# A two-layer Fourier-operator attention kernel: from woven stages to 1748 recorded units issued in one planned order

## The chip, the cores and the metric

The kernel runs on one core of one Trainium2 chip, as a single launch, with all data in float32. The metric is device microseconds of one execution; three executions of the kernel before took 553.83, 553.83 and 556.35 us, median 553.83. The profiled execution is a further one, recorded with the hardware profiler.

## The reference

The input x is 2 images x 56 rows x 128 x 128. Two layers of the same form follow each other, with weights of their own. Each adds to x an attention block on spectral convolutions, applied to a group-normalised x:

```python
def _gn(v, G=32, eps=1e-5):        # mean and variance over 56, 128 and groups of 4 of the last axis
    ...
def spectral_conv(x, w, b):        # keeps 32 x 16 Fourier modes
    xf = jnp.fft.rfft2(x, norm='forward')
    top = jnp.einsum('bihw,iohw->bohw', xf[:, :, :M1, :M2], _c(w[0]))
    bot = jnp.einsum('bihw,iohw->bohw', xf[:, :, -M1:, :M2], _c(w[1]))
    ...
    y = jnp.fft.irfft2(of, s=(H, W), norm='forward')
def fno_layer(x, w, b, sw, sb, norm=False, act=False):
    y = spectral_conv(x, w, b)     # inorm: over an image's 128 x 128 plane, norm only for M0, M1
    if norm: y = inorm(y)
    y = y + skip1x1(x, sw, sb)
    if act: y = jax.nn.gelu(y, approximate=False)
    return y
# the block, on xa = x.reshape(B * K, 1, H, W), K = 56 tokens an image, 8 heads
xn = inorm(xa, g1, b1)
k, q, v = (fno_layer(xn, ...) for K, Q, V)
scores = jnp.einsum('baks,bals->bakl', qh, kh) * scale   # s runs over the 128 x 128 plane
attn = jax.nn.softmax(scores, axis=-1)
out = fno_layer(einsum('bakl,bals->baks', attn, vh) ..., Pw, Pb, Psw, Psb)
att = inorm(out + xa, gan, ban)
an = inorm(att, g2, b2)
h = fno_layer(an, M0w, M0b, M0sw, M0sb, norm=True, act=True)
h = fno_layer(h, M1w, M1b, M1sw, M1sb, norm=True, act=False)
y = inorm(h, gmo, bmo) + att
# the program
x = x + _L0_conv_ref(_gn(x), ...)
x = x + _L1_conv_ref(_gn(x), ...)
```

## The kernel before

**What it computes instead.** K, Q and V are never formed in space. Scores, values and norms are worked out from the 32 x 16 modes of each token and from one 56 x 56 matrix per image, the Gram matrix of the normalised tokens (the sum over the whole plane of products of two tokens). Only the gelu and the result are full planes.

**Tiles.** `X2` [128, 2 images, 64, 128] holds x: two halves of the image rows on partitions 0 to 55 and 64 to 119, and each half has eight spare partitions behind it, which are filled at the start from x; the first of them (56 and 120) later holds a row that carries the bias, written at L564. `P0` and `P1` [128, 8192] are a plane of each image with the last axis on the partitions; P is used again as a room for the attention's parts, and then for h. `WU`, `WT` and `WM` hold the mode matrices of the weights, `tc` their factors, `C` the constants (transform matrices, identity, masks), `xr` three rooms of 1024 columns for x read back from DRAM, `store` a DRAM tensor for x between the layers. PSUM is two pools that rotate: `bank` (2 buffers of 512 columns) and `pair` (3 buffers of 1024).

**The steps**, one function each, for layer L and image b:

- `turned` (L363 and L365 transposes on TensorE, L368 and L371 copies on ScalarE, L373 VectorE's statistics): turns x from X2 into P, eight turnings an image.
- `prepare` (L270 to L302, VectorE and GpSimd): the weights become spectral factors. `relay` (L320 to L335): TensorE transposes, VectorE spreads (L324) and TensorE matmuls move the factors to the partitions of their modes, ScalarE copies them out (L335). `build` (L341, GpSimd, 1024 columns an instruction) and `build_m` (L348) widen them into WU, WT and WM.
- `modes_chain` (L460 to L513): mean and variance, the root on ScalarE (L468, Sqrt) and VectorE's reciprocal, scaling of P in four parts (L479 ScalarE, L481 VectorE), the row transform L485, VectorE's 32x32 transposes L490, the column transform L386, the modes `xf`; L495 writes a 128x1 column for the scale; L505 are two DMAs of `xs`, a copy of the modes on other partitions.
- `gram` (L521): 128 steps an image, each a matmul of 64 weight columns by 56 columns, on two column groups in turn, all into one bank. `gram_chain` (L531 to L554): folding, diagonal, root.
- `scale_x` (L560): VectorE scales X2 in eight pieces of 1024 columns an image, on 120 partitions; L564 are two DMAs that write that extra row.
- `scores` (L588, L607), `values` (L630), `softmax_chain` (L647 to L665), `mix_chain` (L673 to L690), `heads` (L700), `norms_chain` (L712 to L753; ScalarE Square L715, Sqrt L731): the attention on modes; `multiply` (L419), `spread`, `sums` (L441, L443) and `inverse` (L401, L406) are its helpers.
- `gelu`: `synthesis` (L761, inverse transform into two pairs) and `mixed` (L776, the skip from X2); Gelu on ScalarE (L829, 1024 columns), the statistics of h on VectorE (L831, two of 512 columns), transposes L811 (`turn_back`), ScalarE's copy L812, row transform L799 (`forward`), copy L804. Eight such pieces an image.
- `h_chain` (L845 to L890; Sqrt L869, L876): the norms of M1 from modes and from the statistics of h.
- `end`: `synthesis` and `mixed` again, VectorE's `scalar_tensor_tensor` (L926), the residual on GpSimd (L928), stores and loads of x through SyncE's queue (`moved`, L906). In layer 0 `turned` follows piece by piece, for layer 1. In the last image of layer 1 the eight pieces of x are loaded ahead into X2's room of image 0.

**Order.** Each step is a generator that yields a cost in microseconds; `_woven(lead, *bulks)` issues from the bulk until the cost that the lead gave is used up. Engines and buffers are fixed in the code. The main sequence is a fixed list of such pairs, for example, in each layer:

```python
_run(_woven(chain(modes_chain(L, 1, stats[1], s1), more), gram(0, s0)))
build(WTv, tcs, 16, range(0, 8, 2))
build_m(tcs)
_run(_woven(gram_chain(L, 0, s0), _with(gram(1, s1), scale_x(0, s0))))
...
_run(_woven(norms_chain(L, 1, s1), gelu(L, 0, s0)))
_run(_woven(h_chain(L, 0, s0), gelu(L, 1, s1)))
```

Each engine works through its own queue in the order of issue, so this order also fixes each engine's.

Of the kernel before, what the change touches and what calls it, by code (L numbers as in the profile page):

```python
# [22 lines left out]
for _name, _n in (  # L50
    ("ident", N), ("fw", 32), ("fh", N), ("gw", N), ("group", N), ("dup", N), ("ext", N), ("fold", 64),
    ("raw", 56), ("count", 2), ("syn", 1), ("same", 32), ("m8", 8), ("m16", 16), ("n2", 1), ("fx", N), ("gh", 2 * N),
):
    _PARTS[_name] = (sum(n for _, n in _PARTS.values()), _n)
# [3 lines left out]
def _constants():  # L58
# [25 lines left out]
    dup, ext, fold = np.zeros((N, N)), np.zeros((N, N)), np.zeros((N, 64))  # L84
    for r in range(2):
        dup[k, 64 * r + k] = 1
        ext[k, 64 * r + k] = 1
        ext[k, 64 * r + K] = -1
        fold[64 * r + k, k] = 1
# [16 lines left out]
        "ident": np.eye(N), "fw": fw, "fh": fh, "gw": gw, "group": group, "dup": dup, "ext": ext,  # L106
# [4 lines left out]
        "m8": (p[:, None] % 8 == np.arange(8)) * 1.0,  # L111
        "m16": (p[:, None] // 8 == np.arange(16)) * 1.0,
# [3 lines left out]
    return {"all": np.ascontiguousarray(whole, np.float32)}  # L116
# [24 lines left out]
def _woven(lead, *bulks):  # L141

    rest = chain(*bulks)
    for want in lead:
        while want > 0:
            cost = next(rest, None)
            if cost is None:
                break
            yield cost
            want -= cost  # L150
    yield from rest


def _with(bulk, extra):

    for cost in bulk:
        next(extra, None)
        yield cost


def _run(units):
    for _ in units:
        pass
# [3 lines left out]
def fno_layers(ctx: ExitStack, tc: tile.TileContext, x, out, weights, small, const):  # L167
    nc = tc.nc
    V, S, G, T = nc.vector, nc.scalar, nc.gpsimd, nc.tensor
    pool = lambda name, bufs, **kw: ctx.enter_context(tc.tile_pool(name=name, bufs=bufs, **kw))  # L170
    cp = pool("const", 1)
    xp = pool("x", 1)
    pp = pool("plane", 1)
    wp = pool("mats", 1)
    sp = pool("modes", 1)
    sm = pool("small", 1)
    dp = pool("dram", 1, space=bass.MemoryType.DRAM)
    ps = pool("psum", 2, space=bass.MemoryType.PSUM)
    pq = pool("pair", 3, space=bass.MemoryType.PSUM)

    def bank():
        return ps.tile([N, 512], F32, name="bank")

    def pair():
        return pq.tile([N, 2, 512], F32, name="pair")

    def little(name, shape):
        return sm.tile(shape, F32, name=name)
# [3 lines left out]


    Ct = cp.tile([N, N_CONST], F32, name="C")
    C = {k: Ct[:, o : o + n] for k, (o, n) in _PARTS.items()}
    ident = C["ident"]
    nc.scalar.dma_start(out=ident, in_=const["all"][:, :N])
    stage = cp.tile([N, 1632], F32, name="stage")
    nc.scalar.dma_start(out=stage[:, :1088], in_=weights[0].rearrange("p m r n t -> p (m r n t)"))
    smt = [cp.tile([N, N_SMALL], F32, name=f"sm{n}") for n in range(2)]  # L200
    for n in range(2):
        nc.scalar.dma_start(out=smt[n], in_=small[n : n + 1, :].to_broadcast([N, N_SMALL]))
    nc.scalar.dma_start(out=Ct[:, N:], in_=const["all"][:, N:N_CONST])
    X2 = xp.tile([N, B, 64, N], F32, name="X2")
    xin = x.rearrange("b k (g c r) w -> c b k g (r w)", c=2, r=8)
    for b in range(B):
        for g in range(0, 8, 2):
            for c in range(2):
                nc.sync.dma_start(
                    out=X2[64 * c : 64 * c + K, b, 8 * g : 8 * g + 16, :].rearrange("p (g r) w -> p g (r w)", r=8),  # L210
                    in_=xin[c, b, :, g : g + 2, :],
                )
    for b in range(B):
        nc.sync.dma_start(out=X2[K:64, b], in_=x[b, :8, :64, :])
    eps = cp.tile([N, 1], F32, name="eps")
    V.memset(eps, EPS)
    ones = cp.tile([N, N], F32, name="ones")
    V.memset(ones, 1.0)
    P = [pp.tile([N, 8192], F32, name=f"P{b}") for b in range(B)]
    plane = [t[:, : N * K].rearrange("p (i k) -> p i k", i=N) for t in P]  # L220
    WU = wp.tile([N, 4096], F32, name="WU")
    WT = wp.tile([N, 4096], F32, name="WT")
    WM = wp.tile([N, 1024], F32, name="WM")
    WUv, WTv = (t.rearrange("p (t a m) -> p t a m", t=8, a=HEADS) for t in (WU, WT))
    WMv = WM.rearrange("p (n t m) -> p n t m", n=2, t=8)

    FB = [WU[:, 1792 * b : 1792 * b + 1792] for b in range(B)]
    half = [WT[:, 2048 * b : 2048 * b + 2048] for b in range(B)]
    hT = [WT[:, 2048 + 896 * j : 2944 + 896 * j].rearrange("p (r e c k) -> p r e c k", r=2, e=4, c=2) for j in range(2)]
    xr = cp.tile([N, 3, 1024], F32, name="xr")  # L230
    G.memset(xr.rearrange("p a b -> p (a b)"), 0.0)
    store = dp.tile([B, K, N, N], F32, name="store")


    def prepare(layer, first, second):

        sml = smt[layer]
        par = {n: sml[:, o : o + k] for n, (o, k) in _COLS.items()}
        raw = stage[:, :1088].rearrange("p (m r n t) -> p m r n t", m=2, r=2, n=N_W)
        cpt = stage[:, 1088:1376].rearrange("p (n t) -> p n t", t=8)  # L240
        rawc = C["raw"].rearrange("p (k t) -> p k t", k=7)
        W, M = raw[:, 0], raw[:, 1]
        Wf = W.rearrange("p r n t -> p (r n) t")
        der = little(f"der{layer}", [N, 48])
# [8 lines left out]
        tt, ts = second.tensor_tensor, second.tensor_scalar  # L253
        ss, vp = col("ss", 8), col("vp", 8)
        tt(ss, par["s_q"], par["s_k"], ALU.mult)
        tt(vp, par["s_p"], par["s_v"], ALU.mult)
        g2 = col("g2")
        tt(g2, par["g1"], par["g1"], ALU.mult)
        ts(col("score_g", 8), ss, g2, 1.0 / N, ALU.mult, ALU.mult)
        ts(col("mix", 8), vp, par["g1"], None, ALU.mult)  # L260
        tt(col("A0"), par["g2"], par["gan"], ALU.mult)
        tt(col("A02"), d["A0"], d["A0"], ALU.mult)
        tt(col("A0m0"), d["A0"], par["m0sw"], ALU.mult)
        ts(col("gan2"), par["gan"], par["gan"], EPS, ALU.mult, ALU.add)
        ts(col("dc0"), par["m0sw"], par["b2"], par["m0sb"], ALU.mult, ALU.add)
        tt(col("bb"), par["ban"], par["bmo"], ALU.add)
        tt(col("gm1"), par["gmo"], par["m1sw"], ALU.mult)
        tt(col("m12"), par["m1sw"], par["m1sw"], ALU.mult)
        tt(col("m2"), par["m1sw"], par["m1sw"], ALU.add)
        first.tensor_tensor(Wf, Wf, _bc(rawc[:, 0], 1, 2 * N_W), ALU.mult)  # L270
        first.tensor_tensor(M, M, _bc(rawc[:, 1:3], 2, N_W), ALU.mult)
        first.tensor_tensor(W, W, M, ALU.add)
        first.tensor_tensor(W[:, 0, 0:32, :], W[:, 0, 0:32, :], _bc(sml[:, 0:32], 2, 8), ALU.add)
        rooms = (stage[:, 1376:1632], stage[:, 544:800])

        def part(r, n):
            return W[:, r, 8 * n : 8 * n + 8, :]

        def place(e, t64, to, re, im, k):

            n = re.shape[1]
            m0, m1 = _bc(rawc[:, k], 1, n), _bc(rawc[:, k + 1], 1, n)
            u, v = (t[:, :n] for t in t64[2:])
            e.tensor_tensor(u, re, m0, ALU.mult)
            e.tensor_tensor(v, im, m1, ALU.mult)
            e.tensor_tensor(to[:, :, 0], u, v, ALU.subtract)
            e.tensor_tensor(u, im, m0, ALU.mult)
            e.tensor_tensor(v, re, m1, ALU.mult)
            e.tensor_tensor(to[:, :, 1], u, v, ALU.add)

        def product(e, room, o, a, b, conj, minus, scale, k):
            t64 = [room[:, 64 * n : 64 * n + 64].rearrange("p (a t) -> p a t", a=8) for n in range(4)]
            re, im, u = t64[:3]
            e.tensor_tensor(re, part(0, a), part(0, b), ALU.mult)
            e.tensor_tensor(u, part(1, a), part(1, b), ALU.mult)
            e.tensor_tensor(re, re, u, ALU.add if conj else ALU.subtract)
            e.tensor_tensor(re, re, _bc(minus, 2, 8), ALU.subtract)
            e.tensor_tensor(im, part(0, a), part(1, b), ALU.mult)
            e.tensor_tensor(u, part(1, a), part(0, b), ALU.mult)
            e.tensor_tensor(im, im, u, ALU.subtract if conj else ALU.add)  # L300
            for t in (re, im):
                e.tensor_scalar(t, t, scale, None, ALU.mult)  # L302
            place(e, t64, cpt[:, o : o + 16].rearrange("p (a c) t -> p a c t", c=2), re, im, k)
            return t64

        product(first, rooms[0], 0, 1, 0, True, ss, g2, 3)
# [148 lines left out]
    def new_stats(b):  # L455
        return little(f"stats{b}", [N, 16, 6])
# [578 lines left out]
```

## Time and profile before

| | |
|---|---|
| median of three executions | 553.83 us |
| span of the profiled execution | 548.9 us; 4.9 us of the median lie outside a span of this length |
| TensorE (PE) busy | 440.6 us, 80%, 6438 records |
| weight loads (PEld) | 296.4 us, 54% |
| VectorE (DVE) | 350.6 us, 64%, 593 instructions |
| ScalarE (ACT) | 189.6 us, 35%, 238 instructions |
| GpSimd (POOL) | 180.4 us, 33%, 198 instructions |
| DMA | 41.00 MB in 18477 packets; read 24.68 MB, written 14.68 MB |

The span runs from the first instruction to the last. Busy time counts no register, semaphore or DMA-issuing instruction, and the ends of matmuls are modelled, so a busy TensorE is not TensorE at its peak. A float32 matmul shows as two records of TensorE. L926 is line 926 of the kernel before. The page's slices are 40 equal parts of the span with the busy share in tenths; `PEclk` is the granted TensorE clock in the same way. The chain that ended last is followed back from the last instruction, at each step to what released it.

### The profile page before, as it was taken

What the parts mean: (1) busy time and instruction counts of PE and PEld (TensorE: products, weight loads), DVE (VectorE), ACT (ScalarE), POOL (GpSimd) and SP (SyncE); (2) the same over time, 40 slices, a digit from 0 to 9 for tenths busy, and PEclk for the clock granted to TensorE, in tenths of its full rate; (3) what the DMA queues carried; (4) which work ended last, traced back from release to release, by engine and by line L of the source; (5) the groups of instructions that cost most, each with busy time, mean ns of one, the idle gap of its engine ahead of it and who ended that gap; (6) DMA issues with size and microseconds to landing.
All of it is one profiled execution on the core that took longest, in us unless ns stands there. A gap on an engine that the chain in (4) does not pass through costs nothing.

```text
span 548.9 us, 14430 instructions
## 1 busy us (share of the span) xinstructions
PE 440.6 (80%) x6438; PEld 296.4 (54%) x6438; DVE 350.6 (64%) x593; ACT 189.6 (35%) x238; POOL 180.4 (33%) x198
## 2 busy tenths in 40 slices
PE   2548879899989999789688948899998999977480
PEld 1423748768675555445563447577775555534340
DVE  0575579934547676869459994761636867767670
ACT  2333232064545557142102313224546457502000
POOL 2460325900082000155366771440000000044484
PEclk9998797999998999996667958989998999979696
DMA  8992000050000000065144641121000000027597
GB/s 209 220 221 28 10 2 11 7 148 3 2 3 1 1 2 1 1 198 172 51 132 117 187 116 32 13 69 41 4 1 2 1 1 3 1 60 225 181 219 289
DMA packets 18477, 41.00 MB, mean 75 GB/s; under 512 B 4704, under 2 KB 5472, under 8 KB 18400
## 3 DMA queue, kind: packets, MB, share of 16 engines
q1 hardware_dynamic: 17696, 38.71, 26.0%
q10 hardware_dynamic: 720, 1.38, 1.0%
q8 instruction: 50, 0.82, 0.6%
q14 instruction: 11, 0.09, 0.1%
HBM read 24.68 MB, written 14.68 MB: 72 GB/s over the span
## 4 chain that ended last, share of the span: by engine, by line
PE 46%; DVE 30%; ACT 8%; issue 7%; POOL 4%; DMA 3%; POOLq 1%; ACTq 0%; DVEq 0%
PE pair L776 8%; PE pair L761 5%; PE pair L811 5%; DVE X L560 4%; DVE stats L373 4%; PE bank L521 4%; PE bank L700 3%; DMA C<-const_all 3%; DVE P L926 3%; PE bank L485 3%; PE bank L588 3%; PE bank L799 2%; DVE WT L406 2%; PE bank L386 2%; POOL P L928 2%
## 5 line engine op out<-in xcount | busy, mean ns | idle before, releaser
L926 DVE SCALAR_TENSOR_TENSOR P<-P,hs,pair 128x1024 f32<-128x1024 f32 x32 | 40.0, 1268 | 18.8 <-PE pair L776 18.8
L831 DVE BATCH_NORM_STATS2 stats<-P 128x6 f32<-128x512 f32 x64 | 40.5, 680 | 17.3 <-ACT P L829 17.1
L928 POOL TENSOR_TENSOR X<-P,xr 128x1024 f32<-128x1024 f32 x16 | 39.3, 2462 | 32.1 <-DVE P L926 20.2
L373 DVE BATCH_NORM_STATS2 stats<-P 128x6 f32<-128x448 f32 x64 | 35.7, 612 | 20.9 <-ACT P L371 10.6
L560 DVE TENSOR_TENSOR X<-X,gvr 120x1024 f32<-120x1024 f32 x32 | 49.0, 1560 | 0.0
L829 ACT ACTIVATE P<-pair 128x1024 f32<-128x1024 f32 x32 | 32.6, 1026 | 33.0 <-PE pair L776 32.4
L521 PE MATMUL bank<-P 128*64 128x56 f32 (+1 forms) x1024 | 40.5, 250 | 0.0
L776 PE MATMUL pair<-X,Be 57*64 57x512 f32 x256 | 40.1, 726 | 0.0
L521 PEld LDWEIGHTS bank<-P 128*64 128x64 f32 (+1 forms) x1024 | 38.9, 164 | 2.2 <-issue 1.9
L395 POOL MEMSET WT<- 128x256 f32 x4 | 1.3, 314 | 114.5 <-PE bank L799 88.8
L811 PEld LDWEIGHTS pair<-C,P 120*128 120x128 f32 x256 | 27.3, 145 | 21.3 <-issue 11.5
L776 PE MATMUL pair<-X,Bs 57*64 57x512 f32 x256 | 38.4, 641 | 0.0
L761 PE MATMUL pair<-C,WT 32*128 32x128 f32 x512 | 29.3, 336 | 11.1 <-DVE P L926 5.3
L761 PEld LDWEIGHTS pair<-C,WT 32*128 32x128 f32 x512 | 24.0, 229 | 23.4 <-issue 9.3
L811 PE MATMUL pair<-C,P 120*128 120x120 f32 x256 | 35.2, 281 | 0.1
L341 POOL TENSOR_TENSOR WT<-tc,C 128x1024 f32<-128x1024 f32 x8 | 26.5, 3343 | 20.1 <-ACT tc L335 11.0
L812 ACT COPY WT<-pair 128x896 f32<-128x896 f32 x32 | 28.8, 905 | 11.8 <-PE pair L811 11.5
L363 PE MATMUL pair<-C,X 56*128 56x56 f32 x256 | 17.4, 291 | 17.5 <-DMA X<-x 11.9
L371 ACT COPY P<-pair 128x896 f32<-128x896 f32 x16 | 14.4, 901 | 45.7 <-PE pair L365 45.7
L363 PEld LDWEIGHTS pair<-C,X 56*128 56x128 f32 x256 | 14.9, 197 | 24.0 <-DMA X<-x 10.0
L365 PE MATMUL pair<-C,X 120*128 120x120 f32 x128 | 20.3, 312 | 9.2 <-POOL X L928 9.2
L365 PEld LDWEIGHTS pair<-C,X 120*128 120x128 f32 x128 | 16.1, 163 | 21.2 <-POOL X L928 11.6
(260 smaller groups left out, 880.2 us busy)
## 6 DMA issues: line engine op xcount, KB each, us to landing
X<-x SPq DMA_DIRECT2D x16, 448.0 KB
xr<-x SPq DMA_DIRECT2D x32, 224.0 KB
store<-X SPq DMA_DIRECT2D x32, 224.0 KB
out<-P SPq DMA_DIRECT2D x32, 224.0 KB
xr<-store SPq DMA_DIRECT2D x16, 224.0 KB
X<-store SPq DMA_DIRECT2D x16, 224.0 KB
C<-const_all ACTq DMA_DIRECT2D x1, 618.0 KB
stage<-weights ACTq DMA_DIRECT2D x1, 544.0 KB
```

What stands on the lines that cost most here:

```text
L363: T.transpose(p[:, c, o : o + K], X2[q, b, i, :], ident[q, q], tile_position=(64 * c, 0))
L365: T.transpose(p[:, s, N * e : N * e + 120], X2[:120, b, i, :], ident[:120, :120])
L373: V.bn_stats(stats[:, 2 * g + s, :], dst[:, 448 * s : 448 * s + 448])
L521: T.matmul(p[u : u + m, :K], lhsT=P[b][:, K * i : K * i + m], rhs=plane[b][:, i, :], start=(i < 2), stop=(i == N - 1), tile_position=(0, u ...
L560: V.tensor_tensor(v, v, _bc(st["gvr"][:120], 1, 8), ALU.mult)
L761: T.matmul(both[j // 2][:, j % 2, N * e : N * e + N], lhsT=Z[32 * j : 32 * j + 32, o : o + N], rhs=C["gw"][32 * j : 32 * j + 32, :], start ...
L776: T.matmul(p[64 * c : 64 * c + 64, r, :], lhsT=Bs[q, :], rhs=X2[q, b, s : s + 4, :].rearrange("p e w -> p (e w)"), start=False, stop=True, ...
L811: T.transpose(p[:, r, N * e : N * e + 120], h3[:120, o : o + N], ident[:120, :120])
L829: S.activation(h3, both[v].rearrange("p r m -> p (r m)"), AF.Gelu)
L831: V.bn_stats(stats[:, 4 * A + 2 * v + r, :], h3[:, 512 * r : 512 * r + 512])
L926: V.scalar_tensor_tensor(h3, h3, st["hs"], both[v].rearrange("p r m -> p (r m)"), ALU.mult, ALU.add)
L928: G.tensor_tensor(dst, h3, back(n), ALU.add)
```

## The change

The whole scheduling is replaced. The steps no longer issue instructions but write units into a book: each unit is one instruction, or a run of matmuls into one PSUM place, with the engines on which it could run. Lists in the file then give the order of all 1748 units, an engine for each, and a PSUM bank for each place; the units are played in that order under a manual schedule. PSUM is one tile of eight banks.

```diff
+class _Book:
+    ...
+    def play(self, order, chosen, at):
+        for n in order:
+            u = self.units[n]
+            e = chosen.get(n, u.kind[0])
+            for ways in u.calls:
+                op, args, kw = ways[e]
+                args = [self.to_ap(v, at) for v in args]
+                kw = {k: self.to_ap(v, at) for k, v in kw.items()}
+                getattr(self.engines[e], op)(*args, **kw)
+    ...
+_ORDER = (
+    "734F05000s4s8q4p4K5m3X6l063U7I5h07080a090c0b0e0d0Z020V011011120W170f0X0Y1318031a19141b150p161f1c0l1d1e1g1j0h1h"
+    ...
+_ENGINES = (
+    "ADDDDDDDDDDDDDDDDDDDDDDDDDDDVGGGVGGVVGGGVGGVGVVVGVVGVGGVGPVVVPSVVPSVVPSVVPSVVPSVVPSVVPSVVPSVVPSVVPSVVPSVVPSVVP"
+    ...
+_BANKS = (
+    ...
+    with tc.manual_schedule():
+        book.play(*_planned(book))
```

The engine letters are V VectorE, G GpSimd, S ScalarE, P TensorE, and D and A for DMAs issued by SyncE and by ScalarE. Since every instruction is issued from `play`, they all have one line in the profile after (the `getattr` line), and are told apart there by engine, operation and tile.

The steps themselves change in these places. Roots go to GpSimd as a power of -0.5, in place of ScalarE's Sqrt and VectorE's reciprocal:

```diff
-        S.activation(gv, gv, AF.Sqrt, bias=eps)
-        V.reciprocal(gv, gv)
+    def over_root(to, of):
+        G.tensor_tensor(to, of, C["power"][: of.shape[0]].to_broadcast(list(of.shape)), ALU.pow)
+        ...
+        over_root(gv, gv)
```

There are 20 of them. The factors no longer pass through TensorE; they are written to a DRAM tile and read back on other partitions, in four writes and 64 small reads over both layers, on SyncE or ScalarE:

```diff
-            pa = bank()
-            T.transpose(pa[:rows, :N], cpt[:, o : o + n, :].rearrange("p n t -> p (n t)"), ident)
-            ...
+        to = relay[layer][part]
+        dma("DA", to, cpt)
+        ...
+                    dma("DA", tcs[part][q : q + 8], far[c, e_, j])
```

The Gram step becomes two matmuls of 32 weight columns, by 56 and by 28 columns, on four column groups in turn; the part that is left out is the mirror of one that is there, and five small matmuls with the constants "low" and "high" put it together:

```diff
-            T.matmul(
-                p[u : u + m, :K], lhsT=P[b][:, K * i : K * i + m], rhs=plane[b][:, i, :], start=(i < 2),
-                ...
+            u, v = 32 * (i % 4), 32 * ((i + 2) % 4)
+            mm(p[u : u + 32, :K], P[b][:, o : o + 32], P[b][:, o : o + K], i < 2, i >= N - 4, tile_position=(0, u))
+            ...
+            mm(
+                p[v : v + m, K : K + 28], P[b][:, o + 28 : o + 28 + m], P[b][:, o + 28 : o + K], i < 2, i >= N - 4,
+                tile_position=(0, v),
+            )
```

The second moment of h comes from a Square on ScalarE with a running sum, which writes its squares over the PSUM pair that the Gelu read; its mean comes from the modes:

```diff
+                S.activation(h3, flat, AF.Gelu)
+                S.activation(flat, h3, AF.Square, accum_out=sq[:, n : n + 1])
```

Wide elementwise steps are cut into halves of 512 columns that may run on GpSimd or VectorE, and the scaling of X2 now covers the extra rows, since the spare partitions are filled with ones from a constant (four DMAs of together 1 MB):

```diff
-        for s in range(0, 64, 8):
-            v = X2[:120, b, s : s + 8, :]
-            V.tensor_tensor(v, v, _bc(st["gvr"][:120], 1, 8), ALU.mult)
-            ...
+        for s in range(0, 64, 4):
+            v = X2[: 64 + K + 1, b, s : s + 4, :]
+            tt("GV", v, v, _bc(st["gvr"][: 64 + K + 1], 1, 4), ALU.mult)
...
-                G.tensor_tensor(dst, h3, back(n), ALU.add)
+                for r in range(2):
+                    o = slice(512 * r, 512 * r + 512)
+                    tt("GV", dst[:, o], h3[:, o], back(2 * n + r), ALU.add)
+                    if not ahead:
+                        load(2 * n + r + 3)
```

`build` is one instruction for each of the eight parts, on either engine, and WM half as large, built once for each use; `xr` is three rooms of 512 columns that share their space with the weights' stage; the copies out of PSUM may be ScalarE's or VectorE's; the small duplicating matmuls use the identity instead of a constant `dup`. At the start x of image 0 is loaded ahead of the other constants, image 1 behind them. In all, the kernel's counts go from 3558 to 4040 matmuls, from 164 to 273 DMAs issued by SyncE and from 5 to 31 by ScalarE, and from 20 to 4 loads of an activation table.

## The prediction

> **What bounds the kernel now.** I read first the page's engine shares, its slices and its shares of the chain that ended last.
>
> ```profile
> PE 440.6 (80%) x6438; PEld 296.4 (54%) x6438; DVE 350.6 (64%) x593; ACT 189.6 (35%) x238; POOL 180.4 (33%) x198
> ...
> PE   2548879899989999789688948899998999977480
> ...
> PEclk9998797999998999996667958989998999979696
> ...
> PE 46%; DVE 30%; ACT 8%; issue 7%; POOL 4%; DMA 3%; POOLq 1%; ACTq 0%; DVEq 0%
> ```
>
> TensorE is busy 80% of the span, yet it carries less than half of the chain; VectorE carries 30%. The PE digits sag in slices 1 to 4, 17 to 24 and 36 to 40, and the granted clock falls to 0.5 in the second of these. So it is not one engine that is full: there are dense stages and thin ones. The busy times by stage say which:
>
> ```profile
> 105.00:226.00 121.00, 110.76 (x1702) 73.84 (x1697) 74.84 (x153) 63.07 (x78) 21.92 (x53) 0.99 0.07 18
> 226.00:327.00 101.00, 77.78 (x668) 47.93 (x665) 78.80 (x105) 21.48 (x29) 56.92 (x32) 0.75 0.45 129
> 482.00:549.00 67.00, 37.72 (x456) 20.69 (x448) 37.39 (x44) 3.58 (x7) 37.60 (x17) 0.80 0.65 199
> 0.00:42.00 42.00, 16.30 (x177) 11.87 (x180) 19.41 (x56) 13.46 (x14) 18.18 (x67) 1.00 0.91 215
> ```
>
> (window, its length, then busy PE, PEld, DVE, ACT, POOL; clock; DMA share; GB/s.) Attention and gelu of layer 0 (105 to 226) are a PE stage; the end of layer 0 with the modes of layer 1 (226 to 327) has PE and DVE both at 78 of 101 us, taking turns; the first 42 us wait for DMA, and the last 67 for DMA, DVE and POOL.
>
> Busy PE counts latency, so for a floor I take the pace of records back to back, from the chain in order of time (start, us, what):
>
> ```profile
> 97.57 2.87 PE bank L521 x81
> ...
> 171.67 1.10 PE pair L761 x32
> ...
> 257.59 2.35 POOL X L928
> 259.94 9.56 issue
> 269.54 3.85 POOL WU L341 x2
> ...
> 438.88 1.02 PE pair L776 x8
> 439.90 0.97 PE pair L811 x8
> ...
> 442.86 0.52 PE bank L799 x8
> ```
>
> One matmul is two records. Records by pace: L776 512 x 1.02/8 = 65.3; L761 1024 at 1.10 for 32 = 35.2; L811 256 x 0.97/8 = 31.0; the Gram sum L521 1024 x 2.87/81 = 36.3; L607 1024 at 1.08 for 64 = 17.3; L630 18.2, L588 16.0, L700 16.2, L401 16.6, L799 16.6, L365 15.5, L485 13.8, L386 13.2, L363 11.3, L419 8.8, L690 7.7, by the same view; small ones about 20. That is 359, and 13 for the relay matmuls (L320, L331): 372 us, 68% of the span. In 105 to 226 the same sum is 102.5 of 121 us, a fill of 0.85. So 177 us of the span are holes, and most lie outside that stage.
>
> **The change, part by part.**
>
> *PE work.* All but two kinds stay, record for record. The relay goes (13 us, and with it the hole at 260 to 273 where PE waits for POOL's sum and then the build). The Gram sum becomes 1024 matmuls of 32 weight columns by 56 or 28, on four column groups, for 512 of 64 by 56 on two. Lower bound: four lanes for two and 84 columns for 56 per step, 36.3 x 84/56 x 2/4 = 27.2 us. Upper: every record keeps its 35 ns, 72.6. The weight columns per step stay 64, so I take 36.3, no gain. A rule speaks for the upper end: the Trainium skill, TensorEngine Tiling (Array Packing), Instruction Overhead, gives each matmul an overhead of some 60 cycles and says not to tile a dimension that is small already. No run here shows 28 columns; by that rule the sum is that of the rival "split Gram" below. So the floor after is 359.
>
> *ACT.* 20 table loads become 4: 16 x 1.283 = 20.5 us less. Square on ScalarE is new: nearest rows L829 (1.026 for 1024 columns) and L715 (0.58 for 448), so 1.05 each, 32 x 1.05 = 33.6. Of the copies 13 of 32 at L812 (0.905) go to DVE, and 28 DMA issues come at 0.49 (L202's): 13.7. ACT stays near 195. In the gelu stage ACT has 1.03 + 1.05 + 0.54 = 2.6 us for each eighth of a plane, PE 0.55 + 1.02 + 0.97 + 0.52 = 3.06. PE hides it, by 0.4 us only; the PSUM pair is held one Square longer.
>
> *DVE.* Gone: BN statistics of h 40.5, relay spreads L324 8.7, 30.7 of the row scaling (32 at 1.56 become 29 halves at 0.63), half of L804 4.9, small ones 2. New: 20 builds x 0.63 = 12.6, 27 residual halves x 0.63 = 17, 23 evictions of 896 columns at about 1.2 (twice L804's 0.61 for 448) = 27, others 9. 350.6 becomes about 329.
>
> *POOL.* Residual 37 x 1.18 = 44 (it was 76.6), scaling 35 x 1.18 = 41 (new), builds 16 x 1.07 = 17; near 155. The 20 roots are POW on one to three columns. The trace shows no POW: bounds 0.1 us (the smallest POOL row) and 7.9 (its largest, L341); nearest is L495, a 128x1 operation at 0.65, against 0.30 + 0.16 for Sqrt and reciprocal and 1.28 where a table was loaded. I count them at nothing. What they add is a place in POOL's queue, behind TENSOR_TENSORs of 1.07 to 1.18 us.
>
> *SP.* 273 issues for 164. In the end of layer 0: 64 x 0.70 + 32 x 0.355 = 56 us of issuing for 34 before; PE's own 41 us there no longer stand alone, since the turnings of X2 are spread into layer 1's attention in the order. The relay's 68 small DMAs (28 of them ACT's) lie beside PE work. Weights, constants and the rows of ones (1 MB) now lie between the two images, so image 1 lands some 10 us later; image 0's Gram sum covers that, and without that cover it is 10 us. The eight row DMAs at L564 go, as scaling takes the row of ones along.
>
> *The sum.* Head: x of image 0 comes first, 3.67 MB at 215 GB/s = 17 us behind a small constant, and DVE no longer stands behind `prepare` (its statistics ended at 34.0). Last turning and statistics at 22; mean to shift 2.8 as now (34.0 to 36.8); scaling on three engines and four L485 groups 7; Gram sum, cold at first, 9: done at 42, where before it ended at 77. PE work done by then: L363 11.3, L485 3.5, Gram 9, L386 1.7 = 25. Tail: from the first L926 of layer 1 to the end it was 486.8 to 548.9, 62 us. Image 0's pass takes 12, spectrum 20 (23 now, roots without tables), image 1's 15 (POOL 8 x 2.35 = 18.9 now), last DMA and end 7: 54. The bytes alone, 14.7 MB at some 300 GB/s (199 at a share of 0.65), need 49. PE work in it: 37. Between lie 359 - 25 - 37 = 297 us of PE work. One order over all engines means, if it holds, that every stage is filled like the best one: 297/0.85 = 349. Sum 42 + 349 + 54 = 445 of span. The profiled execution is 548.9 of span against a median of 553.83, so 4.9 lie around it: **about 450 us**. Ends: fill 0.95, head 39, tail 48: 405; fill 0.78 with head 42 and tail 55: 483.
>
> **The rivals.**
>
> *The shared port.* Scaling and builds ran beside each other at 88 to 98:
>
> ```profile
> 88.32 10.60 POOL L341 TENSOR_TENSOR WT<-tc,C 128x1024 f32<-128x1024 f32 x4 [11.02 <-ACT tc L335]
> 89.43 7.68 DVE L560 TENSOR_TENSOR X<-X,gvr 120x1024 f32<-120x1024 f32 x3
> ...
> L560 DVE TENSOR_TENSOR X<-X,gvr x32: 1196/1211/3355, 79.1 to 362.8; 120x1024 f32<-120x1024 f32 x32
> ...
> L341 POOL TENSOR_TENSOR WT<-tc,C x8: 1942/2922/7930, 88.3 to 352.0; 128x1024 f32<-128x1024 f32 x8
> ```
>
> Alone they take 1.21 and 1.94 us, together 2.9 each: the sum, not the longer. The change puts 88 such POOL operations beside 76 such DVE ones. If each DVE one waits for a POOL one of 1.1 us, DVE carries 329 + 84 = 413; at a fill of 0.85 that is 486 + 5 = **491**. For it: these rows. Against: the total on both engines, 150 us, is that of before, and the order can keep them apart. The Trainium skill, SBUF — State Buffer, Who interferes with whom, says that this port pair is locked for a whole instruction and the loser blocks; the trace agrees (2.92 for 1.94).
>
> *Split Gram.* Upper bound above: 36.3/0.85 = 43 more, **493**. For it: L443's one-column matmul lasts 0.20 us against L521's 0.25. Against: matmuls on other column groups overlap (eight L799 records of 224 columns in 0.52).
>
> *The plan slips.* Durations differ from those the order was made for, and the fill stays at 0.68: 297/0.68 = 437, + 42 + 62 + 5 = **546**, little gained.
>
> *Slower: roots behind the lock.* A root waits in POOL's queue behind a TENSOR_TENSOR that the port holds up (7.93 at worst), DVE waits for the root, and PE for DVE, with no other PE work ordered in front. 20 x 7.9 = 158: 450 + 158 = **608**. It passes the time of before from 5.2 us a root. For it: L341's maximum and in-order queues. Against: only a few of these rows are over 3 us, and two images give PE other work.
>
> **How the numbers follow.** Forecast 0.60, port 0.13, split Gram 0.07, slip 0.10, slower 0.10. Forecast, port and split Gram hold 0.80: range 405 to 510, the upper end being 493 and half of the step from a fill of 0.85 to 0.78 (32 us), some 510. Runs of this kernel differ by 0.5% (553.83 to 556.35), which is what a measurement can tell. Faster by more: 0.88 (0.02 of the slip lands at no change), same 0.02, slower 0.10.
>
> **What would show it.** In the profile after: statistics of image 0 done near 22 us, Gram done near 42; PE busy near 0.9 from 42 to some 390, clock 0.95 or more there; the last stretch near 54 us; four table loads; DVE near 330, ACT 195. Wrong if: DVE TENSOR_TENSOR rows of 512 columns average over 1.2 us (port); Gram records pace 35 ns each over 2048 (split); PE idles on POOL's POW rows or these last several us (slower); holes as wide as now, on releasers that differ from stage to stage (slip).

## The result, and the profile after

The changed kernel takes 514.24 us (median of four executions, 508.58 to 517.85), the kernel before 555.09 in the same comparison: ratio 0.9293, interval 0.914 to 0.9446. It is faster by 41 us, less than half of the 104 us that the prediction gave, and it lies above the upper end of the range, 510. The profiled execution took 508.58 us with a span of 506.5. Ratios and intervals here leave out executions more than 1.5% above the fastest of their kernel, at a lower granted clock (one of these four, 0.872); medians and ranges have all of them.

The page of the changed kernel, as in the prediction (engine shares, slices, granted clock, shares of the chain):

```profile
PE 383.8 (76%) x7408; PEld 258.3 (51%) x7408; DVE 357.4 (71%) x613; ACT 174.7 (34%) x238; POOL 187.7 (37%) x227
...
PE   2434465889899999995686696996999999954590
...
PEclk9999585999999999997798877988999999996696
...
PE 54%; DVE 24%; issue 8%; ACT 5%; POOL 3%; DVEq 0%; ACTq 0%; POOLq 0%
```

TensorE is busy 57 us less than before, yet it also stands idle 14 us more (506.5 - 383.8 = 122.7, before 548.9 - 440.6 = 108.3). The thin slices still form three groups: 1 to 7, most of 19 to 28, and the last five. "issue", time in which an engine waits for nothing that the profile shows, has 8% of the chain, before 7%. Busy times by stage (window, length, PE, PEld, DVE, ACT, POOL; clock; DMA share; GB/s), cut at the end of the first Gram sum, at the first closing pass, near the start of layer 1's Gram sums, and at the first closing pass of layer 1:

```profile
0.00:58.70 58.70, 20.45 (x668) 15.66 (x670) 25.97 (x70) 9.45 (x9) 17.42 (x55) 0.95 0.78 166
58.70:211.00 152.30, 134.12 (x2669) 91.69 (x2670) 116.91 (x223) 73.78 (x104) 65.03 (x79) 0.94 0.08 17
211.00:276.00 65.00, 49.74 (x625) 29.64 (x626) 56.71 (x82) 15.29 (x18) 34.91 (x32) 0.87 0.55 166
276.00:436.00 160.00, 140.70 (x3001) 100.67 (x2994) 108.80 (x180) 69.92 (x97) 45.70 (x44) 0.91 0.10 30
436.00:506.00 70.00, 38.75 (x474) 20.59 (x466) 49.02 (x62) 6.27 (x11) 24.60 (x19) 0.79 0.68 201
```

Against the sum of the prediction: the first Gram sum ends at 58.65 instead of 42; from there to the first closing pass of layer 1, at 435.96, it is 377 us instead of 349; from there to the end 70.5 instead of 54. Each of the three is 16 to 28 us too long. The waits of TensorE say what is new:

```profile
PE banks L218 <- issue: 27.7, 14, 8.0
PE banks L218 <- DVE P L218: 10.7, 8, 4.0
PE banks L218 <- DMA X<-x: 9.8, 5, 2.9
```

27.7 us of idle TensorE (in 14 pieces, the longest 8.0) have no releaser; in the kernel before, the largest entry of this kind was 3.3. The timeline of TensorE shows the longest of them inside the first Gram sum (start, length, what, count, idle before it):

```profile
39.62 1.55 PE L218 MATMUL banks<-P 128*32 128x56 f32 x130
42.41 1.52 PE L218 MATMUL banks<-P 128*32 128x28 f32 x128 [1.23 <-issue]
47.78 1.52 PE L218 MATMUL banks<-P 128*32 128x28 f32 x128 [3.86 <-issue]
57.27 1.40 PE L218 MATMUL banks<-P 128*32 128x28 f32 x62 [7.97 <-issue]
```

128 matmul records and their 128 weight loads run in 1.52 us, then TensorE stands still, and after exactly as many records again. No data is missing: the last part of P was scaled by 35.9. All 14 holes of the kernel lie so: counted over every record of TensorE in the trace, waiting ones too, they stand whole multiples of 256 apart, to within one record, whatever is computed there. That looks like a block of instructions that arrives late.

### The profile page after: what moved, and what is told of

Its sections match the earlier page's. It is cut to its first block, busy times and chain, and to the rows that moved or that the text cites. A ratio compares the mean times of both kernels' runs of the same rounds, so it can differ in the third digit from the quotient of the medians.

```text
span 506.5 us, 16657 instructions
## 1 busy us (share of the span) xinstructions
PE 383.8 (76%) x7408; PEld 258.3 (51%) x7408; DVE 357.4 (71%) x613; ACT 174.7 (34%) x238; POOL 187.7 (37%) x227
## 4 chain that ended last, share of the span: by engine, by line
PE 54%; DVE 24%; issue 8%; ACT 5%; POOL 3%; DVEq 0%; ACTq 0%; POOLq 0%
PE banks L218 54%; DVE P L218 8%; ACT P L218 3%; DVE WT L218 2%; DVE stats L218 2%; DVE X L218 2%; DVE WU L218 2%; DVE turns L218 1%; DVE dg L218 1%; DVE f L218 1%; DVE M L218 1%; DVE xr L218 1%; DVE vd L218 1%; DVE D L218 1%; DVE sh L218 1%
## 5 line engine op out<-in xcount | busy, mean ns | idle before, releaser
L218 ACT COPY P<-banks 128x896 f32<-128x896 f32 (+4 forms) x64 | 53.3, 856 | 141.8 <-PE banks L218 95.5
L218 PE MATMUL banks<-P 128*32 128x56 f32 (+3 forms) x2656 | 57.1, 220 | 21.7 <-issue 21.0
L218 PEld LDWEIGHTS banks<-P 128*32 128x32 f32 (+1 forms) x2656 | 48.7, 123 | 30.9 <-issue 27.0
L218 PE MATMUL banks<-C,P 32*128 32x128 f32 (+5 forms) x864 | 59.6, 274 | 3.2 <-DVE P L218 1.1
L218 PEld LDWEIGHTS banks<-C,P 32*128 32x128 f32 (+4 forms) x864 | 48.8, 167 | 22.1 <-issue 11.5
L218 POOL TENSOR_TENSOR X<-X,gvr 121x512 f32<-121x512 f32 x35 | 50.5, 1471 | 10.1 <-DVE gvr L218 7.2
L218 DVE SCALAR_TENSOR_TENSOR P<-P,hs,banks 128x1024 f32<-128x1024 f32 x32 | 39.8, 1275 | 14.7 <-PE banks L218 13.2
L218 PE MATMUL banks<-C,X 56*128 56x56 f32 (+1 forms) x384 | 33.0, 290 | 17.6 <-DMA X<-x 9.8
L218 POOL TENSOR_TENSOR X<-P,xr 128x512 f32<-128x512 f32 x22 | 29.3, 1347 | 32.0 <-DMA xr<-x 14.9
L218 ACT ACTIVATE P<-banks 128x1024 f32<-128x1024 f32 x32 | 32.0, 1021 | 22.5 <-PE banks L218 22.4
L218 ACT ACTIVATE banks<-P 128x1024 f32<-128x1024 f32 x32 | 32.9, 1027 | 0.7
L218 PE MATMUL banks<-X,Bs 57*64 57x512 f32 x256 | 33.0, 607 | 0.0
```

Of the source, the lines that this page charges most:

```text
L218: getattr(self.engines[e], op)(*args, **kw)
```

## The experiments

The theories: **1, instruction supply**: the 1024 small matmuls of the split Gram step use up their instructions faster than they are brought in. **2, the shared port**: VectorE and GpSimd hold each other up in the 512-column operations. **3, the order**: the planned order leaves chains of small steps uncovered.

**First: the Gram step of before, in the changed kernel.**

```diff
-            u, v = 32 * (i % 4), 32 * ((i + 2) % 4)
-            mm(p[u : u + 32, :K], P[b][:, o : o + 32], P[b][:, o : o + K], i < 2, i >= N - 4, tile_position=(0, u))
-            ...
+            u, m = 64 * (i % 2), K if i >= N - 2 else 64
+            mm(p[u : u + m, :K], P[b][:, o : o + m], P[b][:, o : o + K], i < 2, i >= N - 2, tile_position=(0, u))
```

> The changed kernel with the Gram step of the kernel before: 512 matmuls of 64 weight columns by 56 on two column groups, in the same units and the same order; half as many instructions in that step. Theory 1, instruction supply: TensorE runs the small matmuls faster (22 ns a record) than its instructions arrive, and stands still after each 256 records; 26 us of such holes are in the profile of the changed kernel (1.23, 3.86 and 7.97 in the first Gram sum alone). With half the instructions the first sum ends near 48 us instead of 58.7, the holes after 256 records are nearly gone, and the profiled span falls from 506.5 to 480 to 492. Theory 2, the port that VectorE and GpSimd share: the Gram step is beside the point, the span stays at 500 to 510. Theory 3, the order itself (chains of small steps that no other work covers): as theory 2, and the saved time comes back as waits on VectorE.

Measured: 486.44 us (486.34 to 490.4), ratio 0.8779 (0.873 to 0.8829), span 484.3. The span is inside the 480 to 492 that theory 1 gave. That is 28 us under the changed kernel, and the intervals are far apart. The waits of TensorE no longer hold an entry for issue at their head, and the timeline of the first sum has no hole:

```profile
PE banks L218 <- DMA X<-x: 14.7, 8, 3.5
PE banks L218 <- DVE P L218: 14.1, 9, 4.0
PE banks L218 <- DVE mv L218: 11.1, 2, 7.2
```

```profile
40.69 1.79 PE L218 MATMUL banks<-P 128*64 128x56 f32 x32
42.41 0.96 PE L218 MATMUL banks<-P,C 128*32 128x448 f32 x8
43.30 6.73 PE L218 MATMUL banks<-P 128*64 128x56 f32 x224
```

The sum ends at 50.0. The page also counts a queue that brings instructions (packets, MB, share), first in the changed kernel, then in this run:

```profile
q8 instruction: 58, 0.95, 0.8%
```

```profile
q8 instruction: 50, 0.82, 0.7%
```

That is eight packets of 16,384 bytes fewer for 512 matmuls fewer, which are 2048 records of TensorE (two matmul records and two weight loads each): 256 a packet. In the traces of the changed kernel and of the first, second, fourth, sixth and ninth experiments no two of these packets start less than 3.3 us apart. The small matmuls use up 256 records in 1.5 us, those of 64 columns in 128 x 30 ns = 3.8. Theory 1 holds. One number of the expectation was misread: the 22 ns came from a count in the chain that lists only part of the records. By the timelines the small matmuls run at 1.52/128 = 12 ns a record and the wide ones at 6.73/224 = 30. So the four split sums are 2048 x 12 = 24 us of TensorE work, against 1024 x 30 = 31 here (36 at the prediction's 35 ns): cheaper than the lower bound of the prediction, 27.2, and the holes of 27.7 us cost more than that gain.

**Second: the same holes without the load of image 1.** The eight DMAs of `load_x(1)` become eight memsets on GpSimd.

> The changed kernel, where image 1 of x is not loaded in layer 0: eight memsets on GpSimd fill its place with constants (its part of the result is left out). The Gram step is that of the changed kernel. Theory 1a, the instructions queue behind data: with the 3.67 MB of image 1 gone from the DMA engines, the holes of 3.86 and 7.97 us in the first Gram sum shrink to the 0.6 to 2.2 us of those in quiet stretches, and the sum ends near 48 to 51 us. Theory 1b, the supply has a fixed pace whatever else is moved: holes as long as before, end near 58. Theory 2 and 3: nothing is said on these holes.

Measured: 506.14 us, one execution, span 504.4. GpSimd's memsets delayed the scaling, so the Gram sum began at 44.4 instead of 37.5; inside it, the timeline reads:

```profile
49.02 1.52 PE L218 MATMUL banks<-P 128*32 128x28 f32 x128 [0.87 <-issue]
52.75 2.45 PE L218 MATMUL banks<-P 128*32 128x28 f32 x128 [2.21 <-issue]
56.21 1.40 PE L218 MATMUL banks<-P 128*32 128x28 f32 x62 [1.00 <-issue]
```

Three holes at the same counts, but 4.1 us in all instead of 13.1. The sum takes 13.2 us instead of 21.2. In the changed kernel the instruction packets before the three restarts start at 40.08, 45.39 and 53.69 and take 0.94, 1.05 and 1.91 us; here they start at 46.40, 50.08 and 53.80 and take 1.25, 1.05 and 0.89. In both, TensorE goes on 1.3 to 1.7 us after each has ended. So there are two parts: a supply that is too slow for 256 records in 1.5 us, and, beside the load of image 1, packets that start late (1a): that of 53.69 starts 4.4 us after the matmuls before it had ended, that of 53.80 here before they had.

**Third: all 512-column operations on VectorE.**

```diff
             e = chosen.get(n, u.kind[0])
+            out = next(iter(u.calls[0].values()))[1][:1]
+            if u.kind in ("GV", "VG") and ...[0] == "tensor_tensor" and int(np.prod(out[0].shape[1:])) == 512:
+                e = "V"
```

> The changed kernel with all TENSOR_TENSORs of 512 columns (scaling of X2, residual, builds) on VectorE; the order is kept. Theory 2, the shared port: the rows of VectorE, 1.03 us on average over 76, fall to their 0.67 alone, and the stalls of 2 to 6.2 us beside GpSimd go. VectorE carries 88 more at 0.67 (59 us) and saves 76 x 0.36 = 27: 357 becomes 389 busy. If the stalls were what the path stood on, the span falls by 5 to 15 us. Theory 3, the order: VectorE is already the engine that the thin stretches wait for, and 32 us more on it cost 10 to 30. Theory 1: no change in the holes after 256 records; no opinion on the rest. I expect 510 to 530 of span.

Measured: 507.63 us (501.55 to 513.2), ratio 0.9074 (0.8999 to 0.9149), 1.3% under the changed kernel by the medians and 2.4% by the ratios, with intervals that touch. The span of 504.2 lies under the 510 to 530 that was expected. What it shows lies in the rows. First those of the changed kernel that scale X2, then the same of this one (min/median/max in ns):

```profile
L218 POOL TENSOR_TENSOR X<-X,gvr x35: 1252/1285/2416, 63.9 to 357.3; 121x512 f32<-121x512 f32 x35
L218 DVE TENSOR_TENSOR X<-X,gvr x29: 664/677/6712, 63.8 to 362.2; 121x512 f32<-121x512 f32 x29
```

```profile
L221 DVE TENSOR_TENSOR X<-X,gvr x64: 664/676/958, 63.1 to 356.5; 121x512 f32<-121x512 f32 x64
...
PE 388.8 (77%) x7408; PEld 260.7 (52%) x7408; DVE 366.2 (73%) x701; ACT 174.7 (35%) x238; POOL 74.2 (15%) x139
```

Beside GpSimd a row of 0.68 us takes up to 6.71. In the changed kernel the 76 wide rows of VectorE sum to 77.1 us, 1.01 each, of which 25 are waiting. With 88 more of them (60 us at 0.68) VectorE is busy only 9 us more, and GpSimd 113 us less: the 25 us of waiting go, and VectorE's other rows sum to 28 us less. What GpSimd took over, VectorE had lost nearly whole. In time the port is worth a few us here, so theory 2 does not explain the miss.

**Fourth: the split Gram step alone, in the kernel before.** The edit is the first experiment's, the other way round; one small DMA brings the constants.

> The kernel before with the Gram step of the change alone (1024 matmuls of 32 weight columns by 56 or 28, four column groups; the two constants for putting it together come by one small DMA an image and layer). Theory 1, instruction supply: records at 22 ns, 45 us for 36, and a hole after every 256 records where the sum runs alone, of 0.6 to 2.2 us in quiet stretches, 16 of them: slower by 10 to 30 us. That the split is cheaper (the lower bound of the prediction, 27 us for 36): faster by up to 9.

Measured: 558.98 us (551.88 to 563.33), ratio 1.0029 (0.9981 to 1.0078): no difference, and the expectation of 10 to 30 us more was wrong. The holes are there all the same, on the same count of 256, but they are fewer (profile of the execution of 563.33 us):

```profile
PE bank L524 <- issue: 4.5, 6, 2.3
PE bank L529 <- issue: 2.1, 1, 2.1
```

```profile
71.53 0.19 PE L529 MATMUL bank<-P 128*32 128x28 f32 x1 [2.12 <-issue]
73.67 0.96 PE L486 MATMUL bank<-P,C 128*32 128x448 f32 x8 [0.89 <-DVE P L482]
```

The first sum, which has the hole of 2.12 us, ends at 77.5 with the split and at 77.1 without. In the order of before its last pieces stand behind row transforms of image 1, and these wait for VectorE's scaling either way: 0.89 us here, 1.62 in the kernel before, where no hole is. The sum also starts at a granted clock of 0.50 (64.2 to 66), where its records come at 18 ns instead of 12. The other three sums were not followed. The same step costs 28 us in one order and nothing that can be measured in the other.

**Fifth: the first and the third edit together.**

> The edits of the first and third experiment together: the Gram step of 64 columns, and all TENSOR_TENSORs of 512 columns on VectorE. Theory 2, the shared port: with the holes in the Gram step gone, the chain between the layers goes through single rows of VectorE that take 4.78 and 4.82 us instead of 0.68 beside GpSimd's; those stalls go, and the span falls from 484.3 (first experiment) to 468 to 476. Theory 3, the order: VectorE's load is the same in both (it rose by 9 us only in the third experiment), and the span stays within 4 us of 484.3.

Measured: 483.78 us (483.21 to 485.17), ratio 0.8733 (0.8663 to 0.8803), span 481.4: 3 us under the first experiment, within the intervals, as theory 3 had it. VectorE's longest wide row is now 2.34 us instead of 6.71, and the time hardly followed.

**Sixth: another order for the fifth experiment's units.** The lists of order and banks are new, the units are not; the search took the durations of the first experiment's profile.

```diff
 _ORDER = (
-    "734F05000s4s8q4p4K5m3X6l063U7I5h07080a090c0b0e0d0Z020V011011120W170f0X0Y1318031a19141b150p161f1c0l1d1e1g1j0h1h"
+    "0807001305060114030V0u0217180b0W0c0Y200Z15210922251j0X10190t1Y110a1n161f1o1k1b0k1X1Z120e0l1p230d0s1a0E0v1m241g"
     ...
```

> The units of the fifth experiment in another order and on other PSUM banks, found by a search over orders that took each operation's duration and the engines from the profile of the first experiment. Theory 3, the order does not suit the chip's durations (the last turnings of image 1 of layer 1 stand behind the closing pass of image 0; the end of layer 0 waits on its own loads): the span falls by 15 to 40 us against the fifth experiment, and most of the gain is in the end of layer 0 and in the tail. Rival, contention is what is left (the granted clock in thin stretches, DMA, the port): within 10 us of the fifth experiment, or slower, because an order made for exact durations suffers from others.

Measured: 459.39 us (456.17 to 462.24), ratio 0.8283 (0.8213 to 0.8353), span 454.0: 24 us under the fifth experiment, the fastest of all. Theory 3 holds: order and banks alone are worth that much on the same units. Whether measured durations or the search itself made the order better is not shown. Lines of its page, and busy times by stage:

```profile
PE   1447948998999999998787998899999999965780
...
PEclk9999977999999999998999999999999999997786
```

```profile
58.00:195.00 137.00, 124.94 (x2248) 85.64 (x2252) 101.55 (x235) 66.87 (x94) 33.38 (x55) 0.96 0.09 18
195.00:260.00 65.00, 54.59 (x771) 33.33 (x766) 62.95 (x103) 15.87 (x19) 10.62 (x14) 0.97 0.37 110
260.00:390.00 130.00, 124.41 (x2316) 87.75 (x2316) 106.50 (x214) 66.82 (x95) 18.65 (x25) 1.00 0.22 65
390.00:454.00 64.00, 38.33 (x482) 20.72 (x474) 52.37 (x77) 7.74 (x12) 2.53 (x4) 0.83 0.75 220
```

Against the fifth experiment, 7 us are gained up to the first closing pass (194.1 for 201.0), 11 from there to that of layer 1 (195.9 for 206.5), and 10 in the tail (64.0 for 73.9). The expectation had most of it in the end of layer 0 and the tail; it is spread more evenly, and the end of layer 0 is now VectorE's, busy 63 of 65 us. The slices with a granted clock under 0.9 are 7, after the change 14.

**Seventh: the recorded order.** The units of the first experiment, played as they were recorded:

```diff
-        book.play(*_planned(book))
+        _, chosen, _ = _planned(book)
+        order = list(range(len(book.units)))
+        ...
+        book.play(order, chosen, at)
```

> The units of the first experiment in the order in which they are recorded, step after step and image after image, with PSUM banks given out anew. It says what the planned order is worth. Theory 3: little is covered any more, the engines' busy times (PE 382, VectorE 357, ScalarE 175) add up in part: 620 to 800 us. Rival, the engines' own queues sort it out and the order matters little: below 530.

Measured: 922.62 us, one execution; TensorE busy 55%, mean granted clock 0.707. The planned order is worth a factor of 1.9 on the same units, more than the 620 to 800 us expected: TensorE's 511 us and VectorE's 376 alone come to 887 of the span of 920.7.

**Eighth: the roots back on ScalarE and VectorE.**

```diff
-        G.tensor_tensor(to, of, C["power"][: of.shape[0]].to_broadcast(list(of.shape)), ALU.pow)
+        G.root(to, of)
+        book.units[-1].calls.append({"G": ("reciprocal", (to, to), {})})
...
+                if op == "root":
+                    self.engines["S"].activation(*args, AF.Sqrt)
+                elif op == "reciprocal":
+                    self.engines["V"].reciprocal(*args)
```

> The changed kernel with its 20 roots as before: Sqrt on ScalarE and reciprocal on VectorE, in the same places of the order. The prediction counted the move to GpSimd at nothing for the chain, and as 16 table loads of 1.283 us less on ScalarE. By that: the table loads come back (about 20), of which those before a root lie on a chain (1.28 + 0.30 + 0.16 for 0.55): 20 x 1.2 = 24 us at most, half of it covered: slower by 5 to 20 us than the changed kernel. The prediction's slower rival (roots held up in GpSimd's queue): faster by 10 or more.

Measured: 521.99 us (517.6 to 525.37), ratio 0.9387 (0.9299 to 0.9476): some 8 us slower than the change, as expected, with touching intervals. GpSimd's rows for the roots in the changed kernel last 0.53 to 2.21 us, 15.8 for all 20.

**Ninth: the split Gram step in the sixth experiment's order.** Edit as in the first experiment, reversed.

> The sixth experiment (new order, wide rows on VectorE) with the Gram step of the change again: 1024 matmuls of 32 weight columns by 56 or 28. Theory 1, instruction supply: the price of the first experiment is found again in another order, 459 becomes 475 to 490, and the profile shows TensorE standing still on nothing but issue for 15 us or more. Rival: the 27 us of the first experiment were a matter of where the old order had put the Gram step; here most of it is covered, 459 to 468.

Measured: 467.29 us (465.42 to 468.04), ratio 0.8388 (0.8351 to 0.8426): 8 us over the sixth, at the edge of the two intervals, and inside the 459 to 468 of the rival, not the 475 to 490 of theory 1. Issue still has 14.9 us of TensorE's idle time, so the supply is short again, but the price is a third of the first experiment's. The timeline suggests why:

```profile
39.61 0.87 PE L221 MATMUL banks<-P 128*32 128x56 f32 x64
40.41 0.71 PE L221 MATMUL banks<-C,X 56*128 56x56 f32 x16
41.04 0.86 PE L221 MATMUL banks<-P 128*32 128x56 f32 x64
41.84 0.70 PE L221 MATMUL banks<-C,X 56*128 56x56 f32 x16
...
50.18 0.74 PE L221 MATMUL banks<-P 128*32 128x28 f32 x25 [4.00 <-issue]
```

This order mixes the small matmuls with the turnings of image 1, where 16 records take 0.71 us and 64 of the small ones 0.87; the same number of instructions is spread over more time. Beside the load of image 1 there are holes even so, of up to 4.00 us.

**Tenth: GpSimd's share of the wide operations in the sixth experiment's order.** The third edit is left out.

> The sixth experiment's order and banks with the engines of the change: 88 of the TENSOR_TENSORs of 512 columns on GpSimd again, beside 76 on VectorE. Theory 2, the shared port, in the form that the third and fifth experiments left of it (what GpSimd takes over, VectorE loses by waiting): within 2% of 459, with VectorE's wide rows at about 1 us and single ones of several us. If GpSimd's help is a real one, 445 to 452; if the stalls fall on a chain here, 470 to 485.

Measured: 495.19 us (492.76 to 497.48), ratio 0.8906 (0.8847 to 0.8965): 36 us over the sixth, beyond the worst of the three expectations (470 to 485). Two rows of it:

```profile
L218 POOL TENSOR_TENSOR X<-X,gvr 121x512 f32<-121x512 f32 x35 | 45.2, 1308 | 0.7 <-PE banks L218 0.7
...
L218 DVE TENSOR_TENSOR WT<-tc,C 128x512 f32<-128x512 f32 x11 | 14.0, 1290 | 0.0
```

A row of X2 that takes 0.68 us on VectorE takes 1.31 on GpSimd, and VectorE's rows of WT beside it 1.29. How much of the 36 us is the port, how much the slower engine and how much an order that does not suit them was not separated.

**Eleventh: only the first Gram sum in the form of before.** Edit as in the first experiment, for layer 0 and image 0 alone.

> The changed kernel where only the first of the four Gram sums (layer 0, image 0, beside the load of image 1) has the 64-column step of the kernel before; the other three keep the change's. The first experiment brought 28 us for all four; of 26 us of holes 13 lie in the first sum. Theory 1 with 1a (instructions queue behind the load of image 1): the first sum alone brings 10 to 16 us, 498 to 504 in time, and ends near 50 us instead of 58.7. Rival (what counts is the count of small matmuls, a quarter each): 5 to 8 us.

Measured: median 504.42 us (495.08 to 506.76), kernel before 554.31, without an interval: under the change by 10 us by the medians and 13.5 by the fastest executions. The spread of 12 us leaves the size loose, so the time does not decide between the two expectations (10 to 16, or 5 to 8). The profile is clearer: TensorE waits 13.6 us on issue in all instead of 27.7, and the first sum ends at 50.8.

The other runs agree on what goes with these holes: issue has 26.0 us in the third experiment and 26.8 in the eighth, which keep the split and the order, and at most 3.0 in the first, fifth, sixth and tenth, which do not have the split.

## Why the prediction was right or wrong

**Right.** The direction; the table loads are four; the tail's first pass takes 12.3 us for 12; the roots are cheap, and the slower rival (608) is refuted by rows of at most 2.21 us and by the eighth experiment. The dense stages do not come up to their model: by the page's busy time they fill TensorE to 0.88, where the stage that gave the 0.85 had 110.76 of 121 us, 0.92, by the same measure.

**Wrong: "Gram sum, cold at first, 9: done at 42".** It took 21.2 us, 13.1 of them holes; the 8.1 left are near the 9. The step that failed is that the supply of instructions was put at nothing. The prediction bounded the split from both sides by column groups and by records (27.2 and 72.6), and neither price was the one that came: a record became cheaper (12 ns) and the supply of instructions became the limit. The rival "split Gram" was given 43 us and a chance of 0.07; by its own mark, 35 ns a record, it was false, and its size was too large (28 us measured). The rest of the head's 17 us is small terms: TensorE waited 9.8 us in all for x of image 0, whose last piece was turned only from 22.3 on, so its statistics ended at 27.0 instead of 22, and mean to shift took 4.3 for 2.8. The prediction's own terms, 22, 2.8, 7 and 9, make 40.8, not 42.

**Wrong: "one order over all engines means, if it holds, that every stage is filled like the best one".** By the prediction's own 297 us of work, the middle was filled to 297/377 = 0.79, 28 us too long. About half of that is the same supply: 14 us of holes (27.7 less the 13.1 of the head), and with the first experiment's edit the middle is 363 us (50.0 to 413.0). With the wide rows on VectorE as well it is 407.5 - 50.8 = 357, a fill of 0.83, though the tail then takes 2.6 us more. So some 8 of the 28 us are left to the order that came with the change. The sixth experiment's order has 332 us there, but some 10 us of TensorE's work moved into its head (busy 32.4 us by 58, in the fifth 22.4 by 50.8): a fill near 0.86. So the fill of 0.85 was in reach of these units. The rival "the plan slips", at 0.68, was far too large for this stage, and its reason, durations other than those the order was made for, is not shown.

**Wrong: the tail, "spectrum 20".** From the last operation of image 0's pass (448.24) to the first of image 1's (482.45) it is 34.2 us; before, it was 15.9 (506.24 to 522.10), since the spectrum then began beside image 0's pass. The chain of the changed kernel shows what was not counted:

```profile
439.73 6.01 PE banks L218 x96
...
449.94 0.92 ACT turns L218
...
452.12 3.67 DVE WT L218 x4
455.84 3.28 PE banks L218 x8
...
478.80 5.92 PE banks L218 x80
```

TensorE does image 0's closing pass first (96 records), and only then the last turnings of image 1; the copy of `turns` at 449.94 and the transposes of WT at 452.12 belong to the gelu stage, and their 11 us came on top of 23 for the spectrum. The lists of the change fix this order, so it could have been read beforehand. In the sixth experiment's order the two passes stand 6.6 us apart and the tail is 64.0 us, so order is a large part of this; the 54 was reached in no run.

**Mis-sized.** VectorE 357 us for 329: the wide rows at 1.01 us instead of 0.63 make 29 of it, which is the port rival in small, and its mark (1.2 us) was not reached. ScalarE 175 for 195: its sum held 13.7 us of DMA issues, which busy time does not count; GpSimd 188 for 155 (its wide rows at 1.35 for 1.18, and 15.8 for the roots). What lies around the span was 2.1 us, not 4.9: the 4.9 set the span of one execution against the time of others, and in the kernel before an execution of 556.74 us has a span of 555.0.

**The range.** The upper cases moved one term at a time: a fill of 0.78 with the head at 42 and the tail at 55. All three ended on the late side together: the supply acts on the head (13 us) and the middle (14), the order on the tail and the middle.

The way back: 514 to 486 by the supply (first experiment), to 484 with the wide rows, to 459 by the order. That this comes near the 450 of the prediction does not confirm its sum: head, middle and tail are 58, 332 and 64 us there, for 42, 349 and 54.

## What to carry to other kernels

Count the instructions that a step needs per microsecond, not only its columns: splitting a matmul into smaller ones can make TensorE wait for instructions, most of all while large loads run, and mixing small matmuls with large ones may soften it: in the order that does so, the price was 8 us. The price of a step is a property of its place in the order: the same split cost 28, 8 and, as far as can be measured, 0 us in three orders. Where a plan fixes the order, read the order itself at the thin places before giving it a general fill, and move the terms of the range together if one cause acts on all.

## What the runs showed of the hardware that was not expected

TensorE's instructions come in blocks, packets of 16,384 bytes for 256 records, never less than 3.3 us apart in six traces. In the changed kernel, where work uses them up faster, holes stand whole blocks apart, 0.6 to 2.2 us long outside the first sum and up to 7.97 beside the load of image 1. The Trainium skill, Runtime: NRT & Kernel Launch, Instruction fetch mechanics, says that instructions are refilled in blocks of 256 and that crossing such a boundary is mostly hidden; the trace agrees on the 256, and disagrees on the hiding where small matmuls follow each other, with 27.7 us in one execution.

A VectorE row of 0.68 us lasted up to 6.71 us beside GpSimd, and taking 113 us of work off GpSimd cost VectorE 9: for operations with two inputs in SBUF, the second engine was hardly one.

The granted clock goes with the fill, but loosely: mean 0.707 in the recorded order (TensorE busy 55%), 0.902 after the change (76%), 0.961 in the sixth experiment (83%), yet 0.894 before (80%). A poorly filled order also makes its matmuls longer: the same units keep TensorE busy 511 us in the recorded order and 382 in the first experiment.
